# One core, four images: where five groups of instructions stand in a hand-ordered Mamba, attention and expert kernel

## The chip, the cores and the metric

The kernel runs on one core of a Trainium2 chip. The core has a matrix engine (PE, TensorE), three engines for elementwise work (DVE is VectorE, ACT is ScalarE, POOL is GpSimd), and DMA queues, here mostly issued from SyncE (SP). The metric is the device time of one launch in microseconds; lower is better. The kernel before took 2177.85 us, the median of three runs (2172.67 to 2179.22).

## The reference, cut to what matters

The input is four images of 256 channels and 32 x 32 pixels, so N = 1024 tokens each, in fp32. Each image goes through a block of a selective scan, gated convolutions and an attention, and then through a layer of experts:

```python
xc = layernorm(x).reshape(B, N, 4, 64)            # four groups of 64 channels
xm = mamba(xc) + skip * xc                        # selective scan over the tokens, 16 states
Q = conv1d(conv1d(x_concat, qdw, groups=4), qpw)  # "qd" and "gp"
xg = sigmoid(Q) * xm                              # the gates
R = conv1d(conv1d(xg, rdw, groups=C), rpw) + xg   # residual: depthwise, then pointwise
cat = concat([xs, R])                             # 2C channels
xm2 = conv1d(conv1d(cat, fdw, groups=2*C), fpw) + xs
x_local = conv1d(xm2, lc, groups=C)
x_global = mha(xm2)                               # 8 heads of 32 channels
x_out = concat([x_local, x_global]) @ fc_w.T      # the joining product "fc"
... layernorm, gelu, 3x3 depthwise convolution, layernorm, projection, added to x
... a layer of 8 experts, the best two for each token, added to the result
```

## The kernel before

**Order.** Nothing is left to a scheduler: every engine executes its instructions in the order in which the program records them, and the program records them tick by tick. Each piece of work is a Python generator that records some instructions and then yields a number of ticks. `beat()` moves all running generators on by one tick. A yield of 1 more therefore puts what follows behind whatever the other generators record in one more tick, on every engine. The helper `in_turn(items, make, use, lag, every)` makes one product every `every` ticks (`make`, on PE) and evacuates it from PSUM `lag` ticks later (`use`, mostly on ACT).

**The scan.** Image by image the selective scan runs in eight parts, a group n of channels (four) by a half h of the tokens (two), each of 16 steps; a step is recorded per tick, so there are 512. A step has: a decay (ACT exp, L715, recorded three steps ahead), an inflow dBu (DVE multiplication of dt*u by bs, L725, into PSUM), the scan itself (DVE, L736), for one half of the tokens a copy of the last state (ACT, L742), and a multiplication by C (POOL, L744). Every fourth step PE makes the next bs (`spread_b`, L707) and adds four finished steps into yp (`sums_of`, L754). At the start of a group PE makes up, zp and dtp, and ACT makes silu (L639, L643), and softplus by exp and ln (L658 to L661), which need another activation table than silu and sigmoid. A table load is an ACT instruction of its own.

**What runs beside it.** While image b is scanned, the convolutions of image b - 1 run in its first half (`convolutions`, L900 to about L1032), and must be done when the fourth part ends (a drain). Then the scan stands still for the attention of image b - 1 until its third step from the end ("attended"). After it, beside the second half of the scan, come `local` and `joined` of that image (the joining product fc, a layer norm, the rest of the block) and, for the image before, `sent_off`: the last norm, the projection, and the dispatch of its tokens to the experts with 16 indirect stores on POOL (L1936). When the scan of image 3 is over, at about 1437 us, its convolutions, its attention and its joining follow beside the first tiles of the experts; from about 1676 us the experts' tiles run alone.

**The convolutions, in their order.** `qd` are twelve products into one PSUM tile (L918); ACT copies it with its bias to SBUF as `qs` (L925); two products of `qs` for each of two chunks c of channels give `gp` (L932); ACT adds a bias (L941) and, after the second chunk, takes the sigmoid of both (L946) and loads the scan's table again; POOL multiplies xm by the gates (L954). Then the residual's depthwise convolution `d` (`depthwise3`): for each chunk a first tap on ACT (L454), and two more on DVE (L459), each of which needs the result before it. The pointwise product `rp` follows, a second depthwise convolution `d4r`, and the product `fp` over four pairs (co, h) of an output chunk and a half of the tokens (`CO_H`, co outermost). ACT evacuates fp into xl (L965), which is xm2. Then `prepared` makes v (`vp`, L1076, evacuated at L1084) and q and k for the attention (`qkp`, L425, evacuated at L1098). `product` is one helper for rp, fp, fc, fx and qkp, so they share the lines L423 and L425.

**The attention.** A block is a group g of four heads and a half h of the queries; its eight steps go over blocks kt of 128 keys, 32 steps in all. In a step PE makes the next step's logits `st` (L1123), ACT takes the exp `e` (L1133), and PE adds the values (`av`, L1172). For the softmax's denominators DVE adds the e of two steps (L1180, a pair), and PE sums the pair over the keys with a product by ones (`sum_pair`, L1144). A step records, in this order: a waiting pair's sum (if kt is odd, or in the last five steps), the next logits, this step's values, and the pair's addition on DVE.

**Buffers.** All products, bs, dBu and yp take their PSUM tile from one pool of eight (tag ps). In SBUF, a8, a4 and a2 tiles (8, 8 and 16 of them) are shared in the same way.

The lines in question are these of `attention`, and the last ones of `joined`:

```python
            for at, (g, h, kt) in enumerate(steps):
                es = ahead
                if pairs and (kt % 2 or at > len(steps) - 6):
                    sum_pair()
                if at + 1 < len(steps):
                    ahead = logits(*steps[at + 1])
...
                ), lag=(4, 4, 2, 2)[b], every=(4, 2, 2, 1)[b],
```

Of the kernel before, what the change touches and what calls it, by code (L numbers as in the profile page):

```python
# [15 lines left out]
C = 256  # L16
# [59 lines left out]
def network(  # L76
# [46 lines left out]
    def col(name, i=0, rows=slice(0, P)):  # L123
        at = _AT[name] + i
        return V[rows, at : at + 1]
# [22 lines left out]
    with tc.tile_pool(name="w_conv", bufs=1) as wp, tc.tile_pool(  # L148
# [291 lines left out]
        def in_turn(items, make, use, lag=2, every=1):  # L440

            made, lag = [], lag // every
            for at in range(len(items) + lag):
                if at >= lag:
                    use(items[at - lag], made[at - lag])
                if at < len(items):
                    made.append(make(items[at]))
                yield every

        CO_H = [(co, h) for co in range(NC2) for h in range(2)]  # L450

        def depthwise3(dst, c, src, c_src, w, wi, bias):

            nc.scalar.activation(  # L454
                dst[:, c, :], src[:, c_src, 0:N], AF.Identity, bias=bias, scale=col(w, 3 * wi)
            )
            yield 1
            for k in (1, 2):
                nc.vector.scalar_tensor_tensor(  # L459
                    dst[:, c, :], src[:, c_src, k : k + N], col(w, 3 * wi + k), dst[:, c, :],  # L460
                    ALU.mult, ALU.add,
                )
                yield 1
# [431 lines left out]
        def convolutions(b):  # L895
# [19 lines left out]
            for k in range(3):  # L915
# [5 lines left out]
                        start=(k == 0), stop=(k == 2),  # L921
                    )
                yield 1 if k else 0
            yield 1
            nc.scalar.activation(qs, qd, AF.Identity, bias=qdw_b)  # L925
            yield 1
            def gate(c):
# [23 lines left out]
            def gating():  # L951
                yield from in_turn(range(NC2), gate, keep)
                for c in range(NC2):
                    nc.gpsimd.tensor_tensor(  # L954
                        xm[:, c, 1 : N + 1], gs[c], xm[:, c, 1 : N + 1], ALU.mult
                    )
                    yield 1
                for c in range(NC2):
                    yield from depthwise3(d[1], c, xm, c, "rdw_w", c, col("rdw_b", c))

            def mixed(at, r):
                co, h = at
# [48 lines left out]
            for c in range(NC2):  # L1011
                for ticks in depthwise3(
# [2 lines left out]
                    next(gated, None)  # L1015
                    yield ticks

            yield from in_turn(
                CO_H, lambda at: product(
                    f"fp_{b}_{at[0]}_{at[1]}", fpwT_s, at[0],  # L1020
                    [
                        d[ci // 2][:, ci % 2, half(at[1])]
# [2 lines left out]
                    xl[:, at[0], ds(1 + at[1] * HALF, HALF)] if beside else None,  # L1025
                    NC2 if beside else 0,
                ), mixed, lag=2 if b == B - 1 else 4, every=1 if b == B - 1 else 2,
            )
            yield from prepared(b)


        def largest(b, g, q, k):  # L1032
# [34 lines left out]
        def prepared(b):  # L1067

            xm2 = XM2[b]
            v8 = a8(f"v8_{b}").rearrange("p c (t x) -> p (c t) x", x=C)  # L1070

            def values(t2):
                vp = ps(f"vp_{b}_{t2}")
                for t in range(2):
                    for ci in range(NC2):
                        nc.tensor.matmul(  # L1076
                            vp[:, ts(t, C)], xm2[:, ci, ds(1 + (2 * t2 + t) * P, P)],
                            wvT_s[:, ci, :], start=(ci == 0), stop=(ci == NC2 - 1),
                        )
                return vp  # L1080

            yield from in_turn(
                range(NK // 2), values,
                lambda t2, vp: nc.scalar.copy(  # L1084
                    v8[:, ds(2 * t2, 2), :], vp.rearrange("p (t x) -> p t x", x=C)
                ),
            )

            qk = [a8(f"qk_{b}_{g}") for g in range(2)]
            OT[b] = [qk[g][:, 0, :] for g in range(2)]  # L1090
            QKV[b] = v8, qk
            yield from in_turn(
                [(g, w, h) for g in range(2) for w in range(2) for h in range(2)],
                lambda at: product(
                    f"qkp_{b}_{at[0]}_{at[1]}_{at[2]}", wqkT_s[:, :, 2 * at[1] + at[0], :], 0,
                    [xm2[:, ci, ds(1 + at[2] * HALF, HALF)] for ci in range(NC2)],
                ),
                lambda at, r: nc.scalar.activation(  # L1098
                    qk[at[0]][:, at[1], half(at[2])], r, AF.Identity,
                    bias=qk_b[:, 2 * at[1] + at[0] : 2 * at[1] + at[0] + 1],  # L1100
                ),
            )

        def attention(b):

            v8, qk = QKV.pop(b)
            rows = [  # L1110
                largest(b, g, qk[g][:, 0, :], qk[g][:, 1, :]) if shifted else None
                for g in range(2)
            ]
            yield 1
            steps = [(g, h, kt) for g in range(2) for h in range(2) for kt in range(NK)]

            def logits(g, h, kt):

                q, k = qk[g][:, 0, :], qk[g][:, 1, :]
                sts = [ps(f"st_{b}_{g}_{h}_{kt}_{i}") for i in range(4)]  # L1120
                for i in range(4):
                    r = ts(i, HD)
                    nc.tensor.matmul(  # L1123
                        sts[i], k[r, ts(kt, P)], q[r, half(h)], start=True, stop=not shifted
                    )
                    if shifted:
                        nc.tensor.matmul(
                            sts[i], ones[HD * i : HD * i + 1, :],
                            rows[g][HD * i : HD * i + 1, half(h)], start=False, stop=True,
                        )  # L1130
                es = [a2(f"e_{b}_{g}_{h}_{kt}_{i}") for i in range(4)]
                for i in range(4):
                    ins = nc.scalar.activation(es[i], sts[i], AF.Exp, scale=1.0 / HD**0.5)  # L1133
                T["exps"] = ins if b == B - 1 else None
                return es

            log_exp()
            ahead = logits(*steps[0])
            pairs, accs, ending = [], [None, None], []

            def sum_pair():
                kt, acc, es = pairs.pop()
                for i in range(4):
                    nc.tensor.matmul(  # L1144
                        acc[ts(i, HD)], ones[:, 0:HD], es[i], start=(kt == 1), stop=(kt == NK - 1)
                    )

            def end_block(g, h, values, total):

                low, out = a2(f"low_{b}_{g}_{h}"), OT[b][g][:, half(h)]  # L1150
                at = (2 * b + g) * 2 + h
                nc.scalar.activation(low, total, AF.Ln, bias=added)
                if shifted:
                    nc.scalar.activation(low, low, AF.Exp, scale=-1.0)
                else:
                    nc.vector.tensor_reduce(sums[:, 0, at : at + 1], total, AX.X, ALU.max)
                    nc.scalar.activation(
                        low, low, AF.Exp, scale=-1.0, accum_out=sums[:, 1, at : at + 1]
                    )
                nc.vector.tensor_tensor(out, values, low, ALU.mult)  # L1160

            for at, (g, h, kt) in enumerate(steps):
                es = ahead
                if pairs and (kt % 2 or at > len(steps) - 6):
                    sum_pair()
                if at + 1 < len(steps):
                    ahead = logits(*steps[at + 1])
                if kt == 0:

                    accs = [ps(f"av_{b}_{g}_{h}_{w}") for w in range(2)]  # L1170
                for i in range(4):
                    nc.tensor.matmul(  # L1172
                        accs[0][ts(i, HD)], v8[:, kt, ts(4 * g + i, HD)], es[i],
                        start=(kt == 0), stop=(kt == NK - 1),
                    )
                if kt % 2 == 0:
                    first = es
                else:
                    for i in range(4):
                        nc.vector.tensor_tensor(first[i], first[i], es[i], ALU.add)  # L1180
                    pairs.append((kt, accs[1], first))
                    if ending:
                        end_block(*ending.pop())
                if kt == NK - 1:
                    ending.append((g, h, *accs))
                if at == len(steps) - 3:
                    T["attended", b] = True
                yield 1
            sum_pair()
            yield 1  # L1190
            end_block(*ending.pop())
            yield 1
# [59 lines left out]
        def joined(b):  # L1252
# [4 lines left out]
            while b == B - 2 and not T.get(("projected", b - 1)):  # L1257
# [7 lines left out]
                ),  # L1265
                lambda at, r: nc.scalar.activation(
                    xc[:, at[0], half(at[1])], r, AF.Identity, bias=fcb[:, at[0] : at[0] + 1]
                ), lag=(4, 4, 2, 2)[b], every=(4, 2, 2, 1)[b],
            )

            T["joining", b] = True
# [1164 lines left out]
```

## Time and profile before

| what | value |
|---|---|
| median of three runs | 2177.85 us |
| profiled execution | 2175.2 us, its span 2173.3 us |
| mean granted PE clock | 0.956 of full speed |
| the three attentions within the scan | 436.2 to 535.4, 795.3 to 892.6, 1191.4 to 1280.9 us |
| end of the scan | 1436.6 us |
| attention lengths, first exp to last exp | 101.6, 100.0, 92.2 and 84.1 us |
| DVE scans (L736) | 512 of 1206 to 1269 ns |
| ACT decays (L715) | 512 of 718 ns |
| POOL multiplications (L744) | 512 of 1340 ns |
| ACT table loads | 1283 ns each |

A part of 16 scan steps with nothing beside it takes about 27 us; one with convolutions beside it takes 29 to 42. The profile is that of one execution, taken by the hardware profiler. "Busy" of PE is modelled at its end, since matmuls are pipelined; weight loads (PEld) have a row of their own. In a line of the timeline the columns are the start in us, the length in us, the engine, the line of the program, the operation, out<-in, the tile's partitions x elements, and how many instructions were joined; the bracket is the idle time of the engine just before and what ended it.

### The profile page before, as it was taken

To read this page: it belongs to the slowest core of one execution; us is meant where nothing else is said; L and a number is where in the kernel's file an instruction comes from. 1 tells how busy PE (TensorE), PEld (TensorE's weight loads), DVE (VectorE), ACT (ScalarE), POOL (GpSimd) and SP (SyncE) were. 2 spreads that over 40 slices of the span, in tenths; PEclk is the share of its full clock that TensorE was granted. 3 is DMA by queue.
4 is the path that set the end of the run, shared out by engine and by line. 5 is a ranking of instruction groups with operands and counts; after the bars stand their busy time and mean duration, and the time that the engine had idled before them with its cause. 6 is when DMAs were issued, how large, how long until landed. Compare 5 with 4: busy or idle time off the path is not lost. (4 is left out here: it accounts for less than half of the span.)

```text
span 2173.3 us, 28179 instructions
## 1 busy us (share of the span) xinstructions
PE 1937.3 (89%) x8690; PEld 867.6 (40%) x8690; DVE 1536.4 (71%) x2231; ACT 1211.4 (56%) x2272; POOL 1042.7 (48%) x930
## 2 busy tenths in 40 slices
PE   6778778999987999988789999679999999999995
PEld 2112112322212332222124223126743668888884
DVE  4989999957998989699898998985364445121111
ACT  4665657668777577776566876524277423222221
POOL 0887887712788850476887026742021113322221
PEclk8888999999999999998999999889999999999997
DMA  3565553401444431154634204344330267866665
GB/s 104 148 156 131 127 123 93 100 28 57 104 117 114 105 73 40 29 138 104 168 81 118 69 22 107 85 164 139 92 82 21 55 189 215 255 182 187 178 159 167
DMA packets 157088, 251.41 MB, mean 116 GB/s; under 512 B 34740, under 2 KB 101332, under 8 KB 156664
## 3 DMA queue, kind: packets, MB, share of 16 engines
q1 hardware_dynamic: 136560, 223.47, 37.6%
q0 software_dynamic: 12720, 17.32, 4.1%
q10 hardware_dynamic: 7640, 8.65, 1.2%
q8 instruction: 72, 1.18, 0.2%
q14 instruction: 96, 0.79, 0.1%
HBM read 137.22 MB, written 36.62 MB: 80 GB/s over the span
## 5 line engine op out<-in xcount | busy, mean ns | idle before, releaser
L744 POOL TENSOR_TENSOR dA<-hs,cs 128x512 f32<-128x512 f32 x512 | 682.0, 1340 | 376.1 <-DVE hs L736 307.6
L715 ACT ACTIVATE dA<-dts,A 128x512 f32<-128x512 f32 x512 | 358.9, 718 | 160.9 <-DMA dts<-dt 66.7
L754 PE MATMUL yp<-dA,quads 128*32 128x512 f32 x1024 | 289.0, 637 | 87.8 <-POOL dA L744 76.0
L2303 POOL DMA_INDIRECT Y<-ys,dest x68 | 109.5, 1610 | 429.6 <-DVE ys L2295 422.5
L1133 ACT ACTIVATE e<-st 128x512 f32<-128x512 f32 x512 | 263.8, 606 | 89.4 <-PE st L1123 88.9
L2268 ACT ACTIVATE hs<-h,b 128x256 f32<-128x256 f32 (+1 forms) x256 | 110.0, 478 | 345.7 <-PE h L2263 233.8
L725 DVE TENSOR_TENSOR dBu<-dts,bs 128x512 f32<-128x512 f32 x384 | 259.6, 677 | 47.4 <-PE bs L707 13.4
L736 DVE TENSOR_TENSOR_SCAN hs<-dA,last,dBu 128x512 f32<-128x512 f32 x192 | 243.6, 1269 | 1.8 <-PE yp L754 1.1
L2276 PE MATMUL y<-w,hs 128*128 128x256 f32 (+1 forms) x1088 | 242.6, 382 | 0.5 <-ACT hs L2268 0.3
L2263 PE MATMUL h<-xT,w 128*128 128x256 f32 (+1 forms) x1024 | 239.6, 390 | 1.1 <-DVE xT L2226 1.1
L736 DVE TENSOR_TENSOR_SCAN hs<-dA,dBu 128x512 f32<-128x512 f32 x192 | 231.6, 1206 | 1.0 <-PE var L435 0.7
L1180 DVE TENSOR_TENSOR e<-e,e 128x512 f32<-128x512 f32 x256 | 168.2, 718 | 77.8 <-ACT e L1133 47.8
L2263 PEld LDWEIGHTS h<-xT,w 128*128 128x128 f32 x1024 | 195.2, 192 | 42.8 <-issue 8.6
L2276 PEld LDWEIGHTS y<-w,hs 128*128 128x128 f32 (+1 forms) x1088 | 197.1, 188 | 37.7 <-issue 10.1
L2226 DVE COPY xT<-xp 128x512 f32<-128x512 f32 (+1 forms) x36 | 23.3, 646 | 250.9 <-PE xp L2222 245.1
L707 PE MATMUL bs<-u,xpwT_s 128*32 128x512 f32 x1024 | 161.2, 660 | 41.3 <-DVE hs L736 18.0
L1123 PE MATMUL st<-qk 32*128 32x512 f32 x1024 | 174.0, 638 | 0.3
L754 PEld LDWEIGHTS yp<-dA,quads 128*32 128x32 f32 x1024 | 50.5, 113 | 303.4 <-POOL dA L744 198.6
L1172 PE MATMUL av<-e,v 128*32 128x512 f32 x1024 | 139.5, 604 | 0.0
L1936 POOL DMA_INDIRECT XS<-XR,to x64 | 65.4, 1021 | 90.3 <-ACT e L1133 53.9
L1123 PEld LDWEIGHTS st<-qk 32*128 32x128 f32 x1024 | 59.5, 183 | 115.3 <-issue 85.6
L1144 PE MATMUL av<-e,every 128*32 128x512 f32 x512 | 85.2, 596 | 2.7 <-DVE e L1180 2.6
(335 smaller groups left out, 2639.1 us busy)
## 6 DMA issues: line engine op xcount, KB each, us to landing
dts<-dt SPq DMA_DIRECT2D x512, 128.0 KB
w<-in_W_dram SPq DMA_DIRECT2D x124, 512.0 KB
cs<-cd SPq DMA_DIRECT2D x512, 64.0 KB
xs<-XS SPq DMA_DIRECT2D x32, 260.0 KB
xd<-xn SPq DMA_DIRECT2D x64, 128.0 KB
xn<-in_x_dram SPq DMA_DIRECT2D x8, 512.0 KB
XL<-xl SPq DMA_DIRECT2D x8, 512.0 KB
xl<-XL SPq DMA_DIRECT2D x4, 1024.0 KB
```

The costliest lines, as they stand in the source:

```text
L707: nc.tensor.matmul(bs[r], xpwT_s[:, n, s : s + 1].to_broadcast([P, 32]), T[b, n, "u"][:, half(h)], start=True, stop=True,)
L715: nc.scalar.activation(dA, T[b, n, h, "dts", g][:, 0, :], AF.Exp, scale=A[:, g, n, q : q + 1])
L725: nc.vector.tensor_tensor(dBu, T[b, n, h, "dts", g][:, 1, :], T[b, n, h, "bs", q], ALU.mult)
L736: nc.vector.tensor_tensor_scan(hs, T[b, n, h, "dA", i], dBu, 0.0 if h == 0 else last, ALU.mult, ALU.add)
L744: nc.gpsimd.tensor_tensor(dA, hs, T[b, n, h, "cs", q], ALU.mult)
L754: nc.tensor.matmul(T[b, n, h, "yp"][ts(g, 32)], quads, T[b, n, h, "dA", q * GD + g], start=False, stop=(q == GS - 1),)
L1123: nc.tensor.matmul(sts[i], k[r, ts(kt, P)], q[r, half(h)], start=True, stop=not shifted)
L1133: ins = nc.scalar.activation(es[i], sts[i], AF.Exp, scale=1.0 / HD**0.5)
L1172: nc.tensor.matmul(accs[0][ts(i, HD)], v8[:, kt, ts(4 * g + i, HD)], es[i], start=(kt == 0), stop=(kt == NK - 1),)
L1180: nc.vector.tensor_tensor(first[i], first[i], es[i], ALU.add)
L2263: nc.tensor.matmul(hp[:, i, :], w1(c, k0 + i), xT[:, c, :], start=(c == 0), stop=(c == NC2 - 1))
L2276: nc.tensor.matmul(yp[ts(k % parts, n), ts(t % 2, C)], hidden(k)[:, ds(t * P, n)], w2(k), start=(k < parts), stop=(k >= NHC - parts),)
```

## The change

The diff touches five places.

1. `attention`: `late` is true for image 2 alone, and only there a pair's sum stands where it stood. In the other three attentions a waiting pair's sum is recorded right after the values of the step that follows the pair.
2. `convolutions`, residual: one more idle tick; then both chunks' first taps on ACT in two ticks, then the four DVE taps in four ticks. Before, each chunk had its ACT tap and its two DVE taps in turn.
3. `convolutions`, gates: the small copy `qs` of images 0 to 2 (`beside`) is recorded one tick later, which puts it behind silu and its table loads on ACT.
4. `joined` of image 1: the four fc products come every four ticks instead of every two.
5. The end of `convolutions`: the fp products go over halves first (`H_CO`). `prepared` is one sequence of values and q, k products, ordered by halves of the tokens, and is moved on tick by tick from the fp loop as soon as its first items have been evacuated, instead of after it. The twelve products follow each other without an idle tick between values and q, k.

```diff
+        H_CO = [(co, h) for h in range(2) for co in range(NC2)]
...
-            yield 1
+            yield 2 if beside else 1
             nc.scalar.activation(qs, qd, AF.Identity, bias=qdw_b)
...
+                yield 1
                 for c in range(NC2):
-                    yield from depthwise3(d[1], c, xm, c, "rdw_w", c, col("rdw_b", c))
+                    nc.scalar.activation(
+                        d[1][:, c, :], xm[:, c, 0:N], AF.Identity, bias=col("rdw_b", c),
+                        scale=col("rdw_w", 3 * c),
+                    )
+                    yield 1
+                for c in range(NC2):
+                    for k in (1, 2):
+                        nc.vector.scalar_tensor_tensor(
+                            d[1][:, c, :], xm[:, c, k : k + N], col("rdw_w", 3 * c + k),
+                            d[1][:, c, :], ALU.mult, ALU.add,
+                        )
+                        yield 1
...
-            yield from in_turn(
-                CO_H, lambda at: product(
+            ready = prepared(b)
+            for n, ticks in enumerate(in_turn(
+                H_CO, lambda at: product(
                     f"fp_{b}_{at[0]}_{at[1]}", fpwT_s, at[0],
...
                 ), mixed, lag=2 if b == B - 1 else 4, every=1 if b == B - 1 else 2,
-            )
-            yield from prepared(b)
+            )):
+                for _ in range(ticks):
+                    if n > 3:
+                        next(ready)
+                    yield 1
+            yield from ready
...
+            def of_half(h):
+                return [(2 * h + t,) for t in range(2)], [
+                    (g, w, h) for g in range(2) for w in range(2)
+                ]
+
+            (v0, qk0), (v1, qk1) = of_half(0), of_half(1)
+            yield from in_turn(v0 + qk0[0:2] + v1 + qk0[2:4] + qk1, make, keep)
...
+            late = b == B - 2
...
-                if pairs and (kt % 2 or at > len(steps) - 6):
+                if late and pairs and (kt % 2 or at > len(steps) - 6):
                     sum_pair()
...
+                if pairs and not late:
+                    sum_pair()
...
-                ), lag=(4, 4, 2, 2)[b], every=(4, 2, 2, 1)[b],
+                ), lag=(4, 4, 2, 2)[b], every=(4, 4, 2, 1)[b],
```

`make` and `keep` in `prepared` are the product and the evacuation that the removed code had for values and for q, k: the same products, instructions and shapes.

More of the change, by code (lines that the diff above doesn't have):

```diff
@@ L1080, in values @@
                 return vp
[L1082 to L1087, printed above, removed]
             qk = [a8(f"qk_{b}_{g}") for g in range(2)]
@@ L1091, in prepared, with make, keep @@
             QKV[b] = v8, qk
[L1092 to L1102, printed above, removed]
+            def make(at):
+                if len(at) == 1:
+                    return values(*at)
+                g, w, h = at
+                return product(
+                    f"qkp_{b}_{g}_{w}_{h}", wqkT_s[:, :, 2 * w + g, :], 0,
+                    [xm2[:, ci, ds(1 + h * HALF, HALF)] for ci in range(NC2)],
+                )
+            def keep(at, r):
+                if len(at) == 1:
+                    nc.scalar.copy(
+                        v8[:, ds(2 * at[0], 2), :], r.rearrange("p (t x) -> p t x", x=C)
+                    )
+                    return
+                g, w, h = at
+                nc.scalar.activation(
+                    qk[g][:, w, half(h)], r, AF.Identity,
+                    bias=qk_b[:, 2 * w + g : 2 * w + g + 1],
+                )
+            def of_half(h):
[4 more added lines that the diff above has]
+            yield from in_turn(v0 + qk0[0:2] + v1 + qk0[2:4] + qk1, make, keep)
         def attention(b):
```

## The prediction

> **What bounds the kernel now.** I read the page's busy shares, its 40 slices, the idle time by group, the windows of each stage, and then the timeline around each place that the diff touches. (The page's chain of waits holds only the last output copy and says nothing here.)
>
> ```profile
> PE 1937.3 (89%) x8690; PEld 867.6 (40%) x8690; DVE 1536.4 (71%) x2231; ACT 1211.4 (56%) x2272; POOL 1042.7 (48%) x930
> PE   6778778999987999988789999679999999999995
> DVE  4989999957998989699898998985364445121111
> ...
> 373.00:407.00 34.00, 31.02 (x101) 10.98 (x102) 30.28 (x36) 22.62 (x45) 26.25 (x20) 0.90 0.46 108
> 407.00:436.60 29.60, 29.60 (x122) 11.94 (x120) 27.54 (x30) 20.23 (x36) 22.91 (x21) 1.00 0.39 95
> 436.60:535.40 98.80, 98.40 (x652) 27.73 (x648) 63.74 (x84) 75.61 (x147) 15.36 (x11) 1.00 0.10 33
> 1676.00:2130.00 454.00, 441.96 (x2016) 359.98 (x2010) 137.17 (x422) 127.21 (x265) 110.89 (x123) 0.99 0.61 170
> ```
>
> PE's 89% is an average over three kinds of stage (a window's columns after its length: PE, PEld, DVE, ACT, POOL busy, clock, DMA share). Up to about 1437 us the scan of 512 steps runs, and each step costs DVE an inflow (0.68) and a scan (1.21 or 1.27): between attentions DVE is the bound, near 90% busy. In the attentions, which the scan stands still for, PE is full (98.40 of 98.80). In the tail, 1437 to 2173, PE is full too (441.96 of 454). So an edit pays in two ways: it closes a DVE gap while the scan runs, or a PE gap in an attention. The gaps that the diff aims at:
>
> ```profile
> 343.42 1.23 ACT L454 ACTIVATE d<-xm,V 128x1024 f32<-128x1024 f32 x1
> 344.68 1.88 DVE L459 SCALAR_TENSOR_TENSOR d<-xm,V,d 128x1024 f32<-128x1024 f32 x1 [3.94 <-ACT d L454]
> ...
> 1075.36 0.69 ACT L925 ACTIVATE qs<-qd,qdw_b 128x512 f32<-128x512 f32 x1 [4.98 <-PE qd L918]
> 1083.71 0.70 DVE L725 TENSOR_TENSOR dBu<-dts,bs 128x512 f32<-128x512 f32 x1 [5.42 <-ACT g L941]
> ...
> 920.78 1.88 PE L425 MATMUL fc<-xloc,fcT_s 128*128 128x512 f32 x4
> 922.50 1.88 PE L425 MATMUL fc<-qk,fcT_s 128*128 128x512 f32 x4
> 925.44 0.70 DVE L725 TENSOR_TENSOR dBu<-dts,bs 128x512 f32<-128x512 f32 x1 [5.27 <-PE bs L707]
> ...
> 527.37 1.04 PE L1144 MATMUL av<-e,every 128*32 128x512 f32 x2 [0.40 <-DVE e L1180]
> 529.50 2.06 ACT L1133 ACTIVATE e<-st 128x512 f32<-128x512 f32 x4 [2.93 <-PE st L1123]
> 440.63 2.50 DVE L1180 TENSOR_TENSOR e<-e,e 128x512 f32<-128x512 f32 x4 [4.43 <-PE av L1172]
> ```
>
> The bracket is the engine's idle time before the instruction and what ended it. Each is one place of three or four, one per image.
>
> **What the Trainium skill says.** "TensorE: Matmul & The Clock Gate", "Architectural detail": ScalarE, VectorE and GpSimdE queues are strict FIFO, and on TensorE only weight loads are pulled ahead. The trace agrees: at 1075.36 ACT stands 4.98 us at the small copy, though the silu behind it could run. "PSUM — Partial Sum Buffer", "Specifications (TRN2)": eight banks of 512 fp32 per partition; all products here share them, so inflow waits for an evacuation (the 5.42 "<-ACT g"). "ScalarE: Activation LUTs", "What ACT_TABLE_LOAD costs": a switch is about 1283 ns of load and a drain on top; the trace has the load (mean 1283 ns), but an exp starts straight after one (337.28 + 1.28, then dA at 338.58), so I price a switch at 1.28 alone.
>
> **The change part by part.** A tick is one turn of the hand-written order, about one scan step while the scan runs. Counts "by order" follow the two kernels' instruction orders with the trace's durations. Sums are made against the profiled execution, 2175.2 us (span 2173.3 and 1.9 around it). The median of the three runs is 2177.85, 2.65 more, which I add at the end.
>
> 1. Residual taps (L454/L459, images 0, 1, 2). Before, each DVE tap stands one tick behind its ACT tap, and the ACT tap stands behind gates, two table loads, sigmoid and softplus. DVE waits 3.94, 4.01 and 4.02 us. After, both ACT taps go first, and the four DVE taps (1.76 each, unchanged in number) stand four to five scan steps later. That wait goes. But the ACT burst remains: gate 1.25, table 1.28, sigmoid 2.00, table 1.28, softplus four at about 0.68, all ahead of the decays that the next scans need; following ACT's order by hand with the trace's durations, the scans themselves then wait some 4.3 us where the stage lost 5.3 before. Gain 1 us each for images 0 and 1 (bounds -1 and +3.9). POOL and SP orders do not move.
> 2. Gates' small copy (L925). It moves behind the silu pair, and the gates of chunk 0 behind one more decay, those of chunk 1 behind two. For images 0 and 1 the copy was not late; nothing is gained, and the late gates are the reason for only 1 us above. For image 2, ACT's 4.98 idle is filled by a table load 1.28, two u 1.26, z 1.06 and a table load 1.28 = 4.88 that now stand behind it. The dBu wait of 5.42 shrinks, with the 4.02 of the tap in the same stage: 9.4 in all, of which the burst keeps about 6. Gain 3.5 (bounds 0 and 6). Added wait: the first gate now stands behind decay 3, whose dt landed only at about 331.95 after its issue at 329.41; dBu is queued behind the gate. Inside the 4.3 above.
> 3. Second image's fc products (L425) every four ticks instead of two. The 5.27 us in which DVE waits for bs hold one whole joining product, the two groups of four matmul records at 920.78 and 922.50, just ahead of spread_b at 924.31. Spaced, that product comes after the next up product and this spread_b: by PE's order, bs ends near 921.8 instead of 925.4. Gain 3.6 (bounds 0, if the other products that move take its place, and 5.3). Moved with them: the normalisation and dispatch of image 0 start eight ticks later, so four more of the sixteen indirect stores (POOL, 1.02 each plus its memset, about 5 us) fall beside the gating of image 2, where POOL has about 7 us spare; two loads on SP stand behind four others each. Cost 1 (bounds 0 and 3).
> 4. Halves (fp, values, qk). Number and size of products unchanged; ticks fall from 28 to 22, so PE gets twelve products back to back. From the last d4r tap to the first logits I count, by order, 53.7 us of PE before and 53.2 after. PE was full there (29.60 of 29.60), so nothing shrinks. But spread_b stands behind those packed products: the three that follow come about 0.5, 1.8 and 4.5 us late for DVE, 6.8, where my same count gives 0.4 before. I cost it at nothing: PE reaches the logits some four ticks ahead of the scan, attention is bound by PE, and DVE idles 4.43 at its start and about 35, 21 and 11 us within the three attentions, so scan work left over runs there. Bounds: -1 and +6.4 an image.
> 5. Late sums (L1144), now in attention 2 only. The order moves only for the last two pairs of a block pair: their sums go from ahead of the next logits to behind the values. The other pairs' sums keep their place on PE: between the values of one step and the logits after the next stands nothing else. In attention 0 the last four steps take 4.99, 3.06, 4.36, 2.45 between first exps, against pairs of 2.07 and 3.13; 4.5 over. In attention 1 the excess is 2.2, in attention 3 0.4. PE's own waits for the sum of two e's are 1.8, 0.8 and 0.4, and a part of ACT's refill comes on top: gain 2.5, 1.2 and 0.4, together 4 (bounds 0 and 7).
>
> Sum: 2 + 3.5 + 3.6 - 1 + 0 + 4 = 12.1 us. 2175.2 - 12.1 = 2163.1; on the median's level 2165.7, taken as 2165. The tail is not touched and is bound by PE; I give it 0, and 3 either way for the different hand-over.
>
> **The rivals.**
> A, slower: the packed products starve the scan. One mechanism, in the stage from d4r to the logits: bs late by 6.4 an image, and not hidden, because `drain` and the attention wait for the whole scan part. Against it, attention starts from PE, not DVE. From 12.1 / 3 = 4.0 us an image it eats all gains; in full 19.2: 2177.85 - 12.1 + 19.2 = 2185.
> B, gains eaten at the gates: the taps and the copy give nothing since ACT's burst is what is late, and the spacing half: 4 + 1.8 - 1 + 0 = 5 at most: 2173. For it: ACT is what ended both waits. Against: 4.98 us of ACT idle at image 2 is real.
> C, all DVE gaps close: taps 3.9 + 3.9, image 2 6, spacing 5.3, sums 6: 25, giving 2153. Against: ACT's work stays.
>
> **How the numbers follow.** Forecast 0.53, A 0.15, B 0.20, C 0.12. A run of this kernel can be told from no change by about 0.3%, 6.5 us: faster is below 2171.3, slower above 2184.4. The forecast's own spread, 2157 to 2173, is from its bounds. Faster: 0.49 of the forecast, all of C, 0.07 of B = 0.68. Slower: 0.08 of A. The rest, 0.24, is the same. C ends at 2150 with 0.05 below; A's upper half lies above 2181; so the range is 2150 to 2181.
>
> **What would show it.** Right: no 4 us DVE wait before the residual taps, the wait at image 2's gate under 3 us, the 5.27 before dBu near 1.5, last attention steps near 2.07 and 3.13 in 0, 1 and 3, attention 2 unchanged, tail within 3 us. Wrong: dBu waits for bs of several us just ahead of each attention with the attention's start later (A), or new waits of scans for decays and gates of the size of those removed (B).

## The result: 1.2% slower

The changed kernel takes 2202.32 us, the median of 6 runs (2197.86 to 2205.64), against 2177.13 us before in the same comparison. The ratio is 1.0122, with a 95% interval of 1.011 to 1.0135: slower by some 25 us. The forecast was 2165, with a range up to 2181.

The busy line of the changed kernel's page (profiled execution, span 2202.2 us) has the same instruction counts as before, and busy times within 11 us of it; the rest of the time is waiting:

```profile
PE 1947.2 (88%) x8690; PEld 871.0 (40%) x8690; DVE 1547.0 (70%) x2231; ACT 1215.3 (55%) x2272; POOL 1045.4 (47%) x930
```

To see where, I took from both traces the end of the last scan (L736, L737 after) of each of the 32 parts, and the gap that an attention leaves between two scans. "Image 1" in a row is the image that is being scanned; beside it run the convolutions of the image before. Some stages, before and as a difference (from these ends; one profiled execution each):

| stage | before, us | after |
|---|---|---|
| first scan's start (loads ahead of it) | 52.8 | +2.3 |
| second part of images 1, 2, 3 (gates and taps beside it) | 41.1, 40.0, 49.8 | +1.5, +1.2, -3.2 |
| third part of images 1, 2, 3 | 34.1, 32.5, 32.5 | -0.4, +1.5, +3.3 |
| fourth part of images 1, 2, 3 (fp, values, q and k beside it) | 30.8 each | +7.1, +6.7, +6.7 |
| scan gap of attentions 0, 1, 2 | 99.2, 97.3, 89.5 | -3.8, +0.7, -0.9 |
| fourth part and the gap behind it together | 130.0, 128.1, 120.3 | +3.3, +7.4, +5.8 |
| fifth and sixth part of image 2 (joining products) | 80.8 | -5.7 |
| seventh and eighth part of image 2 (dispatch) | 74.5 | +9.0 |
| scan's end to the kernel's end | 736.7 | -0.4 |

The fourth parts alone are 20.4 us of the 28.9 by which the spans differ. The gaps behind them give 4.0 of it back, so 16.4 us belong to this stage, and some 12 to the rest of the kernel. Windows of that part in the kernel before, then in the changed one, there cut where the products end (columns: length, then PE, PEld, DVE, ACT, POOL busy, clock, DMA share, GB/s):

```profile
406.90:436.20 29.30, 29.30 (x123) 12.01 (x121) 27.64 (x31) 20.12 (x37) 22.51 (x20) 1.00 0.40 96
```

```profile
409.30:437.80 28.50, 28.50 (x111) 11.79 (x114) 19.48 (x22) 18.32 (x32) 17.01 (x16) 1.00 0.27 64
437.80:446.40 8.60, 7.01 (x34) 1.51 (x26) 8.49 (x10) 3.66 (x7) 6.20 (x5) 1.00 0.45 110
```

Both have PE full while products last. Before, DVE is busy 27.64 of 29.30 us, and scan and products end together. After, DVE gets 19.48 of 28.50, and then 8.6 us more follow in which PE has no q, k product left and DVE (8.49 of 8.60) catches up. The timeline of DVE in the changed kernel shows what it waited for in that stage:

```profile
415.72 0.70 DVE L726 TENSOR_TENSOR dBu<-dts,bs 128x512 f32<-128x512 f32 x1 [1.05 <-PE bs L708]
425.91 0.70 DVE L726 TENSOR_TENSOR dBu<-dts,bs 128x512 f32<-128x512 f32 x1 [2.85 <-PE bs L708]
430.50 0.70 DVE L726 TENSOR_TENSOR dBu<-dts,bs 128x512 f32<-128x512 f32 x1 [2.71 <-ACT qk L1120]
434.28 0.70 DVE L726 TENSOR_TENSOR dBu<-dts,bs 128x512 f32<-128x512 f32 x1 [1.90 <-ACT qk L1120]
```

8.5 us, half for bs itself and half for a PSUM tile that a q, k product held. The reason is in PE's order. These are the bs and the q, k products on PE, before and then after:

```profile
413.70 0.62 PE L707 MATMUL bs<-u,xpwT_s 128*32 128x512 f32 x2
...
426.70 1.06 PE L707 MATMUL bs<-u,xpwT_s 128*32 128x512 f32 x8
...
428.56 7.14 PE L425 MATMUL qkp<-xl,wqkT_s 128*128 128x512 f32 x16
```

```profile
424.71 1.06 PE L708 MATMUL bs<-u,xpwT_s 128*32 128x512 f32 x8
...
431.54 5.42 PE L425 MATMUL qkp<-xl,wqkT_s 128*128 128x512 f32 x12
436.89 1.06 PE L708 MATMUL bs<-u,xpwT_s 128*32 128x512 f32 x8
```

Before, the part's last bs stands ahead of the last four products (7.14 us), so DVE finishes the scan while PE finishes the products. After, every product stands ahead of the last bs, and DVE's last four steps can only start when PE is done.

The attention's start is held up too. Here is PE from its last q, k product to the third step's logits of attention 0, before and then after:

```profile
435.62 1.07 PE L754 MATMUL yp<-dA,quads 128*32 128x512 f32 x8
436.62 2.93 PE L1123 MATMUL st<-qk 32*128 32x512 f32 x16
...
440.36 1.44 PE L754 MATMUL yp<-dA,quads 128*32 128x512 f32 x8
441.73 1.14 PE L1123 MATMUL st<-qk 32*128 32x512 f32 x8
```

```profile
437.77 2.68 PE L755 MATMUL yp<-dA,quads 128*32 128x512 f32 x14
441.36 1.04 PE L755 MATMUL yp<-dA,quads 128*32 128x512 f32 x2 [0.92 <-POOL dA L745]
442.34 2.27 PE L1152 MATMUL st<-qk 32*128 32x512 f32 x10
445.26 2.29 PE L1152 MATMUL st<-qk 32*128 32x512 f32 x6 [0.65 <-DVE hs L737]
...
448.94 1.95 PE L755 MATMUL yp<-dA,quads 128*32 128x512 f32 x8
450.82 1.30 PE L1152 MATMUL st<-qk 32*128 32x512 f32 x8
```

In PE's order the scan's sums (yp) stand ahead of the first logits, and now their multiplications on POOL are late (0.92). The second step's logits then wait for PSUM tiles that the scan's last inflows hold (0.65): the first two steps' logits take 5.2 us instead of 2.93. The last yp stands between the second and the third step's logits, as before. From its last q, k product to the third step's logits PE takes 13.9 us, where it took 6.0. From the exps' starts, the second step of attentions 0, 1 and 2 takes 6.78, 8.29 and 6.77 us, where it took 3.19 before. The gaps in the table are hardly longer all the same, because the first exp now starts 2.9 us before the scan's end instead of 1.6 behind it.

### The profile page after: what moved, and what is told of

It is laid out like the page before. It is cut to its first block, busy times and chain, and to the rows that moved or that the text cites. A ratio compares the mean times of both kernels' runs of the same rounds, so it can differ in the third digit from the quotient of the medians.

```text
span 2202.2 us, 28180 instructions
## 1 busy us (share of the span) xinstructions
PE 1947.2 (88%) x8690; PEld 871.0 (40%) x8690; DVE 1547.0 (70%) x2231; ACT 1215.3 (55%) x2272; POOL 1045.4 (47%) x930
## 5 line engine op out<-in xcount | busy, mean ns | idle before, releaser
L737 DVE TENSOR_TENSOR_SCAN hs<-dA,last,dBu 128x512 f32<-128x512 f32 x192 | 243.7, 1269 | 3.4 <-POOL dA L745 2.3
L737 DVE TENSOR_TENSOR_SCAN hs<-dA,dBu 128x512 f32<-128x512 f32 x192 | 231.8, 1207 | 1.3 <-PE av L1174 1.3
L1152 PE MATMUL st<-qk 32*128 32x512 f32 x1024 | 180.2, 643 | 3.4 <-DVE hs L737 3.1
L726 DVE TENSOR_TENSOR bs<-dts,bs 128x512 f32<-128x512 f32 x128 | 86.2, 673 | 0.9 <-DMA dts<-dt 0.9
```

What stands on the lines that cost most here:

```text
L726: nc.vector.tensor_tensor(dBu, T[b, n, h, "dts", g][:, 1, :], T[b, n, h, "bs", q], ALU.mult)
L737: nc.vector.tensor_tensor_scan(hs, T[b, n, h, "dA", i], dBu, 0.0 if h == 0 else last, ALU.mult, ALU.add)
L1152: nc.tensor.matmul(sts[i], k[r, ts(kt, P)], q[r, half(h)], start=True, stop=not shifted)
```

## The experiments

Kernels that ran together share their runs of the kernel before. Ratios are to it, with 95% intervals.

### Part five alone, and the other four without it

`halves` is the kernel before with the fp, values and q, k hunks of the diff; `nohalves` is the changed kernel without them.

> The kernel before with the fifth part of the change alone (fp by halves, values and q, k packed and moved on from the fp loop). Theory P (the packed products make the scan of the fourth part of each image wait, and the end of that scan is what the attention's PE order waits for): slower by 20 to 25 us, about 2200, with the fourth parts at 37 us instead of 29.3. Rival R (the loss needs the later taps and gates of the same change to push the convolutions late; the packing alone is hidden behind PE's work): within 5 us of before.

> The changed kernel with the fifth part undone (parts 1 to 4 kept). Theory P: 2175 to 2181, since the other four parts sum to about nothing by the two traces (taps and gates +1 to +2 in images 1 and 2, fc spacing +3, sums about -4). Rival R: about as slow as the changed kernel, 2195 or more. My recorded sum for these parts, -12, would give 2165.

Measured: `halves` 2208.67 us, ratio 1.0138 (1.0114 to 1.0162), slower than the whole change. The fourth parts are each 5.25 us longer, 36.1 us where theory P had 37; its total is above what was expected. `nohalves` 2192.34 us, 1.0076 (1.0052 to 1.0099): neither text met it. The fourth parts are 1.8 us shorter than before in it, so the fourth parts' loss is part five's; but the other four parts, taken for a near zero, lose some 16 us too. And the parts don't add up: 32 and 16 are together more than 25.

The fourth parts are not all of the loss of `halves`. Its span is 34.7 us longer, and fourth parts and gaps hold 14.7 of that. The third parts of images 2 and 3 hold 8.0: without the later taps of the whole change, PE starts the first values 6.9 us before the end of the third part instead of 1.7, and DVE meets two waits there, for tiles held by other products, that the kernel before does not have (shown for image 1; 2.37 and about 0.6 in the other two):

```profile
397.79 0.70 DVE L726 TENSOR_TENSOR dBu<-dts,bs 128x512 f32<-128x512 f32 x1 [1.84 <-ACT u L640]
401.92 0.69 DVE L726 TENSOR_TENSOR dBu<-dts,bs 128x512 f32<-128x512 f32 x1 [0.59 <-ACT v L1103]
```

The tail holds 5.3, since part five also moves image 3's convolutions, which run there: attention 3 starts 10.4 us earlier after the scan's end, and what follows its start takes 15.8 longer. Most of the rest lies in parts beside which nothing had changed.

### Is it bs, or the tiles?

```diff
-            if g == 1 and q + 1 < GS:
+            if g == (0 if b and at % 8 in (2, 3) else 1) and q + 1 < GS:
                 spread_b(b, n, h, q + 1)
```

> Part five alone, and beside it bs (spread_b) recorded one step earlier in the third and fourth part of images 1 to 3, so that it stands ahead of one more packed product on PE. Theory P1 (late bs is what DVE waits for): the fourth parts fall from 37 to 33 us or less, 8 to 12 us less than the run of part five alone. Theory P2 (the PSUM tiles held by products that PE has not reached are what DVE waits for, the waits ended by ACT's evacuation of q, k): no gain, or a loss of up to 6 us, since bs then holds its tile a step longer.

Measured: 2209.1 us, 1.0149 (1.0132 to 1.0167), no gain; the fourth parts are 5.6 us longer than before. DVE's waits in that stage with part five alone, and then with bs one step earlier (timelines of DVE):

```profile
411.35 0.70 DVE L726 TENSOR_TENSOR dBu<-dts,bs 128x512 f32<-128x512 f32 x1 [0.97 <-PE bs L708]
421.52 0.70 DVE L726 TENSOR_TENSOR dBu<-dts,bs 128x512 f32<-128x512 f32 x1 [2.84 <-PE bs L708]
427.88 0.70 DVE L726 TENSOR_TENSOR dBu<-dts,bs 128x512 f32<-128x512 f32 x1 [2.71 <-ACT xm L785]
```

```profile
419.06 0.70 DVE L726 TENSOR_TENSOR dBu<-dts,bs 128x512 f32<-128x512 f32 x1 [2.73 <-ACT qk L1108]
426.59 0.70 DVE L726 TENSOR_TENSOR dBu<-dts,bs 128x512 f32<-128x512 f32 x1 [1.96 <-ACT qk L1108]
430.36 0.70 DVE L726 TENSOR_TENSOR dBu<-dts,bs 128x512 f32<-128x512 f32 x1 [1.89 <-ACT qk L1108]
```

The waits for bs are gone, and waits for a tile that an unfinished q, k product holds stand in their place; over the stage 7.9 us against 7.6. So neither name in the bracket is the cause by itself: both are what PE's backlog looks like from DVE. No run gave these products PSUM tiles of their own, which would tell the backlog from a mere lack of tiles.

### Order, overlap, packing

Three kernels take part five apart. `fp_order` changes only `CO_H` to `H_CO` for fp. `halves_after` keeps the order and the packing and drops the overlap (26 ticks):

```diff
-            )):
-                for _ in range(ticks):
-                    if n > 3:
-                        next(ready)
-                    yield 1
+            )):
+                yield ticks
             yield from ready
```

`halves_spaced` keeps order and overlap and puts six idle ticks between the remaining products (28 ticks, as before):

```diff
-            yield from ready
+            for n, ticks in enumerate(ready):
+                yield ticks
+                if n % 5 < 3:
+                    yield 1
```

> The kernel before with only the order of the four fp products changed to halves first, nothing overlapped or packed. Theory Q: within 3 us of before, 2174 to 2180. Rival: 2185 or more.

> Part five alone, but values, q and k start only after the fp loop has ended, as before; they stay packed without idle ticks. If the overlap with the fp loop is what backs PE up, most of the loss goes: fourth parts near 30 us, 2180. If it is the packing of the twelve products itself: fourth parts at 35 us or more, 2195 or so.

> Part five alone, with fp by halves and the overlap of values, q and k with the fp loop kept, but with six idle ticks put back between the remaining products, so that the stage has 28 ticks again instead of 22. Theory Q (a packed product per tick is more PE work per scan step than DVE work, so the scan is held to PE's pace while products stand ahead of it, and its last steps then run with PE empty): the fourth parts come back to 29 to 31 us, the second exp of the attentions to about 3.2 us, total 2174 to 2182. Rival (the order by halves or the overlap itself does it): fourth parts stay at 34 us or more, 2195 or more.

| run | ticks | us | ratio (95%) | fourth parts against before, us | with the gap behind them |
|---|---|---|---|---|---|
| `fp_order` | 28 | 2176.80 | 1.0000 (0.999 to 1.0011) | 0.0, -0.5, 0.0 | 0.0, -0.5, 0.0 |
| `halves_spaced` | 28 | 2181.10 | 1.0014 (1.0002 to 1.0026) | +0.65, +0.66, +0.66 | -0.2, -1.9, -0.2 |
| `halves_after` | 26 | 2183.06 | 1.0024 (1.0011 to 1.0037) | +3.8 each | +1.3, +2.9, +1.3 |
| `halves` | 22 | 2208.67 | 1.0138 (1.0114 to 1.0162) | +5.25 each | +2.8, +6.0, +6.0 |

The order costs nothing. The fewer ticks the same products get, the longer the fourth part; with the ticks back, nine tenths of the loss are gone, although the overlap is still there. Theory Q holds for the fourth parts. The overlap isn't quite free: with `halves_spaced` the two waits of the third part (2.4 to 3.0 us together) are there in all three images, and with `halves_after`, which drops the overlap, in none. With `halves_spaced`, the fourth part of image 1 reads

```profile
409.40:440.80 31.40, 31.40 (x130) 11.52 (x128) 28.32 (x31) 20.33 (x37) 23.61 (x21) 1.00 0.35 84
```

PE is as full as in the other two, and DVE gets 28.32 of 31.40 us, where it got 19.48 of 28.50 in the changed kernel while products lasted. One miss: the second step of its attentions takes 5.8, 4.2 and 5.8 us and not 3.2.

### The other four parts, one by one

Each is the kernel before with that part of the diff alone.

> The kernel before with the residual's taps spread (part 2) alone. Theory G (the small copy's move, not the taps, makes the gates late in images 1 and 2): the 4 us waits of DVE before the taps go and no gate wait comes, 3 to 4 us less in each of images 0 and 1, 1 to 4 in image 2: 2166 to 2172. Rival (the taps moved later push the rest of the convolutions later and the fourth parts or the attention's start give it back): 2174 to 2182.

> The kernel before with the small copy one tick later (part 3) alone. Theory G: a new wait of DVE for the first gate of 2 to 4 us in images 0 and 1, and 2 to 3 us less in image 2: plus 2 to 5 us, 2179 to 2182. Rival (the copy costs nothing in images 0 and 1): 2172 to 2175.

> The kernel before with the second image's joining products every four ticks (part 4) alone. From the two traces of before and changed: the sixth part of image 2 gets 4 to 6 us shorter (its wait for bs goes), the seventh and eighth together 5 to 6 longer, the first of image 3 1 to 2 longer: plus 2 to 3 us, 2179 to 2181. My recorded step gives minus 2.6, 2174.5.

> The kernel before with the pairs' sums early in attentions 0, 1 and 3 (part 1) alone. From the exps' intervals of the changed kernel: 1 us less in attention 0, 2 more in attention 1, 1.5 less at most in attention 3, whose gain the tail may take back: 2176 to 2178, no change. My recorded step gives minus 4, 2173.

| run | us | ratio (95%) |
|---|---|---|
| `taps` | 2186.16 | 1.0041 (1.0028 to 1.0054) |
| `qs` | 2180.43 | 1.0014 (1.0004 to 1.0023) |
| `fc` | 2177.22 | 0.9999 (0.9988 to 1.001) |
| `sums` | 2175.32 | 0.9995 (0.9983 to 1.0007) |

`taps`: both expectations were too low. The wait of 4 us before the taps is gone and no wait for a gate came; the second parts of images 1 to 3 are 1.8 to 2.0 us shorter. About 1.8 us of DVE work has moved into each third part, though, and by the end of the attention that follows the lead is gone: over second part, third part, fourth part and attention the sums are -0.8, +1.7 and +1.0 us for the three images. That explains why it gains nothing, not why it loses some 9 us. In this run's profile the rest lies in two parts beside which nothing had changed (+2.8 and +2.0; the first of them is as much longer in the run of the sums alone) and in the tail (+4.0, behind the last attention, where the experts run alone). One profiled execution can't say whether these belong to the change; this stays open.

`qs`: the total and the new wait are those of theory G. ACT and DVE in the changed kernel, at image 0's gates:

```profile
334.31 0.72 ACT L716 ACTIVATE dA<-dts,A 128x512 f32<-128x512 f32 x1 [3.02 <-DMA dts<-dt]
334.94 0.17 ACT L743 COPY last<-hs 128x1 f32<-128x1 f32 x1
335.02 1.26 ACT L942 ACTIVATE g<-gp,V 128x512 f32<-128x512 f32 x2
```

```profile
335.74 0.70 DVE L726 TENSOR_TENSOR dBu<-dts,bs 128x512 f32<-128x512 f32 x1 [3.60 <-ACT g L942]
```

The gate was moved behind one more decay, that decay waits 3.02 us for dt's DMA, and dBu waits 3.60 for the tile that the gate frees. With the copy alone moved the same wait is 3.60 too; before it was 0.22. But in that run it costs little: the wait before the taps falls from 3.94 to 0.93, and the second parts of images 1 and 2 are only 0.4 and 0.1 us longer. It costs once the taps are moved as well, since their wait is then gone already: the taps alone make these parts 1.9 and 1.8 shorter, taps and copy together (in `nohalves`) 1.5 and 1.2 longer. So the mechanism of theory G shows in the pair; where the copy alone loses some 3 us is not shown.

For image 2 the copy helps as meant, 3.0 us in the second part of image 3's scan, and the third part is 3.2 us longer: 1.9 us of DVE work has moved into it, and its wait for bs on PE is 2.52 instead of 1.17. The gain lasts one part.

`fc`: the total is that of the kernel before; both figures of the expectation missed it. With the products spaced, one wait of 2.02 us, for a tile that a joining product held, stands in place of the 5.27 for bs, and the norms and the dispatch of image 0, now later, take it back. DVE with part four alone:

```profile
919.75 0.69 DVE L725 TENSOR_TENSOR dBu<-dts,bs 128x512 f32<-128x512 f32 x1 [2.02 <-ACT xc L1266]
...
1005.80 0.70 DVE L725 TENSOR_TENSOR dBu<-dts,bs 128x512 f32<-128x512 f32 x1 [1.50 <-ACT u L639]
1010.04 0.43 DVE L1809 BATCH_NORM_STATS2 st<-XR 128x6 f32<-128x256 f32 x1 [2.42 <-ACT XR L1794]
```

The last two are not there in the kernel before. The sixth part of image 2 is 4.4 us shorter, the eighth 5.2 longer, and the first three of image 3 are 1.6 to 1.7 longer each. The expectation had the shorter sixth part as the wait that goes, but that wait stood in the fifth, which is 2.4 shorter. What the sixth part loses is work: DVE's instructions other than the scan's fall from 9.7 to 5.0 us there, and rise by 3.3, 2.1 and 1.7 us in the eighth part and in the first two of image 3.

`sums`: no change, as expected. Attention 0 gets 1.4 us shorter (first exp to last, 100.16 for 101.6), attention 1 two longer (101.99 for 100.0), attention 3 1.5 shorter (82.57 for 84.1). What is late next is the exps' own SBUF tile. ACT in this run, at the ends of attentions 0 and 1:

```profile
537.85 0.60 ACT L1133 ACTIVATE e<-st 128x512 f32<-128x512 f32 x1 [1.90 <-PE av L1145]
```

```profile
897.29 1.57 ACT L1133 ACTIVATE e<-st 128x512 f32<-128x512 f32 x3 [3.04 <-PE av L1145]
```

The last step's exp waits for a pair's sum (L1145 in that run); PE has the step's logits ready before that sum, so what the exp lacks is a tile that the sum still reads. A sum that comes later on PE also keeps its e tiles longer.

### What was left of it

`combo` is the kernel before with the sums early in attentions 0 and 3 alone, and with the second image's third and fourth joining products two ticks later:

```diff
+            late = b in (1, 2)
...
-                if pairs and (kt % 2 or at > len(steps) - 6):
+                if late and pairs and (kt % 2 or at > len(steps) - 6):
...
+                if pairs and not late:
+                    sum_pair()
...
-            yield from in_turn(
+            for n, ticks in enumerate(in_turn(
...
-            )
+            )):
+                yield ticks + (2 if (b, n) == (1, 1) else 0)
```

> A version meant to keep what the runs showed as gains: sums early in attentions 0 and 3 alone (1 to 1.5 us each by the exps' intervals), and of the second image's joining products only the third and fourth two ticks later, so that bs passes them (about 3 us of a wait of 5.27) while the dispatch comes two ticks later instead of six or more. If gains stay: 2171 to 2174. If the dispatch takes back what the joining gives, as in the run of part four alone: 2175 to 2178.

Measured: 2171.65 us, ratio 0.9975 (0.9965 to 0.9985): some 5 us faster than the kernel before, and within the first expectation. In its trace the sixth part of image 2 is 4.0 us shorter and the eighth 1.9 longer, against 4.4 and 5.2 with the even spacing. Which of the two edits gains, and how, is not shown: they were not run apart, the sixth part again loses DVE work to later parts (9.7 to 6.3 us), and in the fifth part the wait for bs falls from 5.27 to 1.83, but a new one of 2.97 follows it, so that this part is only 0.5 shorter.

## Why the prediction was wrong

The step that failed is the fourth, the halves, where I wrote "I cost it at nothing". Its count was near: PE's work did not shrink, and DVE was to wait 6.8 us where 8.5 were measured in image 0. What failed is the cover, "scan work left over runs there" in the attention's idle DVE time. PE does finish its products earlier in the part, by 1.9 us. But in its own order the scan's last sums stand ahead of the logits, and the next logits need tiles that the scan's last inflows hold, so PE waits for the late scan: 13.9 us from its last product to the third step's logits instead of 6.0. Fourth parts and gaps together cost 3.3, 7.4 and 5.8 us, 16.4 against the nothing of the forecast. Rival A had this mechanism and its place, and its price, 19.2 for three images, is near that; I had given it 0.15. Its total, 2185, is 17 us too low because it kept the 12.1 us of gains.

These gains are the rest of the miss. The four parts that were to gain them lose some 16 us when they run without the halves. By terms:

1. Taps: the waits went, as said; 1 us each for images 0 and 1 was to remain. The run alone loses some 9 us. That the burst on ACT keeps the scans waiting showed (1.13 twice and 0.89 us in image 1's part), but the gain that I left over is gone by the attention that follows. With the copy moved too, DVE's waits in the second part go from 5.3 to 6.9 us in image 0 and from 4.2 to 5.5 in image 1; I had some 4.3 left in image 0.
2. Small copy: "Inside the 4.3 above" was the wrong term. The decay that waits for dt's DMA, with the gate queued behind it, is a wait of 3.60 us of its own in image 0, which the moved taps no longer cover. In image 2, the 3.5 came (3.0 with the copy alone), and the next part took it back.
3. Joining products: -3.6 was near (5.27 to 2.02, 3.25). The later norms and dispatch, priced at 1 with a bound of 3, took it back: in the parts that only kernels with this edit have longer, the eighth of image 2 and the first of image 3, +5.2 and +1.6. The -5.7 of the fifth and sixth part is mostly work that went there.
4. Sums: -2.5, -1.2 and -0.4 were -1.4, +2.0 and -1.5 in the attentions' lengths. The term that was missing is the exps' wait for e tiles, which a later sum holds longer. PE's waits alone were counted.

That the tail would not move (0, 3 either way) held in number (-0.4), and in part by luck. It is not untouched: image 3's convolutions and attention run in it with parts one, two and five of the change, and with part five alone it is 5.3 us longer.

Beyond single terms, the sum took every DVE gap that closes for time won. Around the convolutions it is not: with the copy alone, the second, third and fourth parts and the attention of image 3 go -3.0, +3.2, -1.5 and +1.9, together +0.6. DVE work moves into the next part, the wait for the next bs grows, and the attention starts no earlier, since PE has to work off the same products before it. I read this from the stages of one trace; no run changed PE's work to test it. Open too is why the parts don't add up: the four without the halves cost 16, the halves alone 32, all five 25. By the stages of the profiles the excess of 21 us lies mostly in the third parts of images 2 and 3 (8.0), the tail (7.7) and the sixth part of image 3 (5.3).

## What to carry to other kernels

Where two streams share an engine in a fixed order, idle slots in one stream are not waste if the other stream's small instructions must pass: the same products in 22 ticks instead of 28 made each fourth part 5.25 us longer, and the bracket named now bs, now a tile, while the backlog was one. Before costing a delay at nothing because another engine is idle later, check that the delayed instructions are recorded there at all, and what stands behind them in the order of the other engines. And of a moved step follow all that it frees: here a sum freed e tiles, a gate freed a PSUM tile, a joining product started a dispatch. A stage that gets shorter may only have handed its work to the next: compare the work in it, and not the length alone.

## What was not expected of the hardware

Nothing in its mechanisms. Most stages that no edit touches agree within 0.1 us from kernel to kernel (28.31 us, for instance, from end to end of a part with nothing beside it), so a table of stage ends shows effects of 1 us that totals, spread over some 14 us from run to run (2170.86 to 2185.33 in 59 runs of the kernel before), don't. But a few stages jump by 1.5 to 3 us in kernels whose edits lie elsewhere (the seventh part of image 2 by 2.8 to 3.1 in the runs of the halves, taps, copy and sums alone), so a single difference of that size in one profiled execution proves nothing.
